# Two graph layers on one core: one fixed order of search matmuls in every attention step, and four smaller moves

## The chip, the core and the metric

The kernel runs on one core of a Trainium2 chip. The core has a matrix engine (TensorE, PE in the profile; its weight loads are listed as PEld), three engines that read and write on-chip memory (VectorE = DVE, ScalarE = ACT, GpSimd = POOL) and a queue (SyncE = SP) that issues all transfers of this kernel. Matrix products land in PSUM, which has eight banks of 512 fp32 columns; everything else lies in SBUF. Each engine takes its instructions strictly in the order of its own list and meets the others through semaphores.

The metric is the device time of one execution in microseconds (us). The kernel before was timed three times: 15735.61 us in the median (15734.61 to 15738.93).

## The reference

The inputs are `x` (3327 nodes x 128), a 0/1 matrix `adj` (3327 x 3327) and weights. There are two residual layers, each followed by a layer norm over the 128 features.

```python
# layer 0
cos = beta * (x @ x.T) / (|x| |x|^T + 1e-7)
x = layernorm(x + softmax(cos + (1 - adj) * -1e9) @ x)
# layer 1: n = 3327, d = 128 heads, h = 8 features per head
q, k, v = [(x @ W.T).reshape(d, n, h) for W in (Wq, Wk, Wv)]
a = softmax(einsum('dnh,dmh->dnm', q, k) * d**-0.5 + adj + adj)
x = layernorm(x + einsum('dnm,dmh->dnh', a, v).reshape(n, h*d) @ Wo.T)
```

Layer 1 dominates: 128 heads, each with a 3327 x 3327 score matrix that is built from only eight features.

## The kernel before

**Tiling.** Nodes are padded to 3328 = 26 tiles of 128 (`T` = 26). Query nodes are taken in nine blocks of three tiles (`QB` = 384 columns; the ninth has two tiles, 256 columns). A *unit* is one block times four heads; there are 9 x 32 = 288 units. A *step* is one unit times one tile of 128 key nodes, so a unit has 26 steps and the kernel has 7,488, of which 6,656 are full (384 columns). Each head's q and k carry 32 rows (eight features split into high and low parts and doubled), so the four heads of a unit lie in the four 32-row groups of PE, and products of different heads can run in PE at the same time. Those of one head share a row group and follow each other.

**Stages.** Layer 0 takes the first 718 us or so. It also turns each tile of `adj` and stores the turned tile to DRAM as `aT_s` (line 215, `adj_chunk`); the tile in SBUF has one buffer. Then a preparation stage (`prepare`, lines 794 to 823, 16 calls: eight groups of heads, k and q) loads 1.66 MB of q or k (`nat`, line 796), reorders it on POOL (798), transposes it on PE, splits it and writes it back (818). The attention loop (lines 872 to 943) runs from about 988 us to 15615 us, and a final stage multiplies with Wo, adds the residual and norms (lines 949 to 983).

**One step of the loop.** PE runs, in this order: the shift products of two heads (`shifts`, L690) into the two-bank tile `e_b`; a search; the score products of those heads (`scores`, L696); the shift products of the other two heads into two single-bank tiles `e_a`; another search; their scores; eight products that add 2 x adj to `e_a` (`add_adj`, L677); eight products that weigh the values of the step two earlier into `acc` (`weigh`, L707). ACT takes the exponential of `e_b` (L893) and of both `e_a` (L923). For the heads of `e_b`, adj is not added before the exponential: POOL multiplies by exp(2 adj) afterwards (L894).

**The searches.** Softmax needs each query row's maximum before its unit begins. So beside the steps of the running units PE forms the scores of the *next two* units only to find their maxima: per step a *pair* (two heads, 512 keys each, into the two-bank tile `m2`, L598, reduced by one DVE instruction, L613) and a *single* (one head, into `m1`, L634). `m2` and `m1` have one buffer each, so the next pair waits for the pair's reduction, and the next single for the single's. `max_steps` (568) writes the list of 52 pairs and singles for two units; 52 steps make a *round*. The list runs 33 steps ahead (`AHEAD` = 7): step s works on search place k = (s + 33) mod 52. Pairs take heads (0, 1) at places 0 to 12, (2, 3) at 13 to 38, (0, 1) at 39 to 51. Line 882 calls a place *early* when its pair has heads (0, 1). An early place runs the pair in the first slot (before the scores of `e_b`) and the single in the second; the others run the single first and the pair second. `e_b` always has heads (2, 3) and `e_a` (0, 1). Two pairs, at places 12 and 26, are made of four products of 256 keys for both units of the round (branch from line 618).

**Around the loop.** When a unit's 26 steps have been weighed, `take` copies `acc` (L718). At step 20 of the next unit (line 916) `values_turn` turns it on PE (L725) and `finish` (735) copies it out on ACT (L737), takes a reciprocal on DVE (L741), scales on POOL (L742) and stores to `o_s`. At place 26 or 51 (line 928) `shift_parts` reduces the maxima on DVE (L648) and splits them on POOL; three small turns (L663) at steps 22 to 24 bring them to PE's shape. A unit's k and q are loaded (`load_unit`, 517) two units ahead. For each new block, 26 turned adj tiles are loaded (`load_adj_tile`, 505) and exponentiated on ACT (L514).

**Who sets the order.** In layer 0 and layer 1 the lists of PE, ACT, DVE and POOL stand as written (`manual_schedule`). The SP list, and all lists in the final stage, are ordered by a scheduler.

**The final stage.** Per tile: load 128 rows of `o_s` and the residual, eight transposes, two copies (DVE and ACT), eight products, one DVE add into `hid` (978). After the 26 tiles `layernorm` (129) runs over all of them; the scheduler has put the statistics into the tile loop, the square root and 26 scalings (L141) behind it, and the whole output is then written.

## Time and profile before

| | us |
|---|---|
| median of three timed runs | 15735.61 |
| profiled execution, its own time | 15731.62 |
| its span on the core | 15729.8 |
| attention loop, first to last exponential L893 | 988.4 to 15613.0 |
| preparation stage | about 718 to 988 |
| final stage | about 15615 to 15729.8 |
| mean full step | 2.005 |
| mean step of the ninth block | 1.538 |

How to read it: the span is counted from the first instruction that the profile shows. A line such as "4143.72 0.50 PE L598 MATMUL m<-kx,qx ... x1" of the timeline is start, duration, engine, source line, operation, output and inputs, and how many equal instructions are merged; square brackets give idle time before it and what ended that. Matmuls are pipelined, so their shown durations overlap. Step times are differences between successive starts of the exponential L893, of which each step has one. "L141" is line 141 of the kernel.

### The profile page before, as it was taken

To read this page: it belongs to the slowest core of one execution; us is meant where nothing else is said; L and a number is where in the kernel's file an instruction comes from. 1 tells how busy PE (TensorE), PEld (TensorE's weight loads), DVE (VectorE), ACT (ScalarE), POOL (GpSimd) and SP (SyncE) were. 2 spreads that over 40 slices of the span, in tenths; PEclk is the share of its full clock that TensorE was granted. 3 is DMA by queue.
4 is the path that set the end of the run, shared out by engine and by line. 5 is a ranking of instruction groups with operands and counts; after the bars stand their busy time and mean duration, and the time that the engine had idled before them with its cause. 6 is when DMAs were issued, how large, how long until landed. Compare 5 with 4: busy or idle time off the path is not lost.

```text
span 15729.8 us, 508048 instructions
## 1 busy us (share of the span) xinstructions
PE 15442.3 (98%) x217532; PEld 6909.7 (44%) x217532; DVE 13882.2 (88%) x16261; ACT 12687.4 (81%) x24930; POOL 13894.1 (88%) x9571
## 2 busy tenths in 40 slices
PE   8879999999999999999999999999999999999999
PEld 6644444444444444444444444444444444444555
DVE  7679999999999999999999999999999999998775
ACT  7658888888888888888888888888888888888776
POOL 0059999999999999999999999999999999999886
PEclk9989999999999999999999999999999999999999
DMA  4451111111111111111111111111111111111112
GB/s 169 180 201 49 45 49 52 49 46 49 52 50 49 47 50 52 49 45 49 52 49 46 49 53 48 50 45 56 45 49 45 49 52 49 46 49 60 61 56 74
DMA packets 600521, 951.50 MB, mean 60 GB/s; under 512 B 283090, under 2 KB 515408, under 8 KB 557808
## 3 DMA queue, kind: packets, MB, share of 16 engines
q1 hardware_dynamic: 598256, 918.99, 18.0%
q8 instruction: 1703, 27.90, 0.7%
q14 instruction: 562, 4.60, 0.1%
HBM read 784.19 MB, written 134.61 MB: 58 GB/s over the span
## 4 chain that ended last, share of the span: by engine, by line
PE 91%; DVE 2%; ACT 1%; issue 0%; POOL 0%; DMA 0%; SPq 0%; ACTq 0%; DVEq 0%; POOLq 0%
PE acc L707 29%; PE ea L677 20%; PE m L598 15%; PE eb L690 12%; PE ea L690 9%; PE ea L696 2%; PE eb L696 2%; PE ea L663 1%; DVE mx L613 1%; PE ea L725 1%; DVE mx L634 1%; ACT pa L923 0%; PE pp L977 0%; POOL pb L894 0%; ACT pb L893 0%
## 5 line engine op out<-in xcount | busy, mean ns | idle before, releaser
L894 POOL TENSOR_TENSOR pb<-pb,eT 128x768 f32<-128x768 f32 (+1 forms) x7488 | 13206.6, 1781 | 752.7 <-ACT pb L893 557.7
L613 DVE TENSOR_REDUCE mx<-m 128x2 f32<-128x1024 f32 x6784 | 8271.6, 1219 | 506.9 <-PE eb L696 283.1
L893 ACT ACTIVATE pb<-eb 128x768 f32<-128x768 f32 (+1 forms) x7488 | 5895.6, 787 | 2509.9 <-PE eb L696 1716.6
L598 PE MATMUL m<-kx,qx 32*128 32x512 f32 (+1 forms) x23296 | 6774.5, 471 | 85.9 <-DVE mx L613 78.2
L923 ACT ACTIVATE pa<-ea 128x384 f32<-128x384 f32 (+1 forms) x14976 | 6339.0, 478 | 56.5 <-PE ea L677 43.5
L707 PE MATMUL acc<-pb,vt 128*9 128x384 f32 (+1 forms) x29952 | 5904.2, 474 | 0.1
L707 PE MATMUL acc<-pa,vt 128*9 128x384 f32 (+1 forms) x29952 | 5903.3, 474 | 0.0
L634 DVE TENSOR_REDUCE mx<-m 128x1 f32<-128x512 f32 x6400 | 4377.6, 684 | 682.2 <-PE m L598 316.3
L690 PEld LDWEIGHTS <-one 3*128 3x128 bf16 x29952 | 1508.1, 91 | 5553.9 <-issue 4650.8
L677 PE MATMUL ea<-aT,two 128*32 128x384 bf16 (+1 forms) x59904 | 3716.2, 325 | 0.0
L696 PE MATMUL eb<-qx,kx 32*128 32x384 f32 (+1 forms) x14976 | 3444.5, 452 | 0.0
L696 PE MATMUL ea<-qx,kx 32*128 32x384 f32 (+1 forms) x14976 | 3439.1, 437 | 0.0
L690 PE MATMUL ea<-cx,one 3*128 3x384 bf16 (+1 forms) x14976 | 3293.0, 322 | 2.3
L598 PEld LDWEIGHTS m<-kx,qx 32*128 32x128 f32 x23296 | 2813.9, 182 | 443.7 <-DVE mx L613 123.0
L690 PE MATMUL eb<-cx,one 3*128 3x384 bf16 (+1 forms) x14976 | 2462.7, 326 | 1.3 <-ACT pb L893 0.6
L707 PEld LDWEIGHTS acc<-pa,vt 128*9 128x9 f32 x29952 | 1416.7, 91 | 781.5 <-issue 0.3
L677 PEld LDWEIGHTS <-two 128*32 128x32 bf16 x59904 | 947.0, 95 | 1415.6 <-issue 1273.6
L696 PEld LDWEIGHTS eb<-qx,kx 32*128 32x128 f32 x14976 | 1461.7, 189 | 0.0
L696 PEld LDWEIGHTS ea<-qx,kx 32*128 32x128 f32 x14976 | 1433.1, 182 | 8.0 <-issue 3.0
L707 PEld LDWEIGHTS acc<-pb,vt 128*9 128x9 f32 x29952 | 1418.8, 91 | 0.6 <-POOL pb L894 0.6
L638 DVE TENSOR_REDUCE mx<-m 128x2 f32<-128x512 f32 x1088 | 747.9, 687 | 96.3 <-PE eb L696 38.2
L116 POOL MEMSET raw<- 128x1 f32 x26 | 2.4, 98 | 559.0 <-DVE mn L260 478.2
(126 smaller groups left out, 5253.8 us busy)
## 6 DMA issues: line engine op xcount, KB each, us to landing
kx<-kp_s SPq DMA_DIRECT2D x576, 832.0 KB
vn<-v_s SPq DMA_DIRECT2D x288, 416.0 KB
qx<-qp_s SPq DMA_DIRECT2D x1024, 48.0 KB
raw<-in_adj_dram SPq DMA_DIRECT2D x25, 1663.5 KB
aT_s<-aT SPq DMA_DIRECT2D x26, 832.0 KB
aT<-aT_s SPq DMA_DIRECT2D x208, 96.0 KB
q_s<-row SPq DMA_DIRECT2D x26, 512.0 KB
k_s<-row SPq DMA_DIRECT2D x26, 512.0 KB
```

The costliest lines, as they stand in the source:

```text
L598: nc.tensor.matmul(dst, u.qx[rows(a), q * P : (q + 1) * P], u.kx[rows(a), k0:k1], start=True, stop=True,)
L613: nc.vector.tensor_reduce(u.mx[:, h, qs[0], c], m, axis=AX.X, op=ALU.max)
L634: nc.vector.tensor_reduce(u.mx[:, a, qs[0], c : c + 1], m, axis=AX.X, op=ALU.max)
L638: nc.vector.tensor_reduce(u.mx[:, a, qs[0] : qs[1] + 1, c], m.rearrange("p (q k) -> p q k", q=2), axis=AX.X, op=ALU.max,)
L663: nc.tensor.matmul(dst[r], parts[u.i % 2][:, q, h], unit, start=start, stop=True, tile_position=(0, 32 * h), skip_group_check=True,)
L677: nc.tensor.matmul(e[r, : u.nq], two[:, r], aT[:, j, : u.nq], start=False, stop=True, tile_position=(0, 32 * c), skip_group_check=True,)
L690: nc.tensor.matmul(e[:, : u.nq], one[r], u.cx[r, : u.nq], start=True, stop=False, skip_group_check=True)
L696: nc.tensor.matmul(e[:, : u.nq], u.kx[rows(a), j * P : (j + 1) * P], u.qx[rows(a), : u.nq], start=False, stop=stop, skip_group_check=True,)
L707: nc.tensor.matmul(acc[32 * h : 32 * h + H + 1, : u.nq], u.vt[:, h, j], pts[h // 2][:, h % 2, : u.nq], start=(j == 0), stop=(j == T - 1), ...
L893: nc.scalar.activation(pt_b[:, :, : u.nq], e_b[:, :, : u.nq], AF.Exp)
L894: nc.gpsimd.tensor_tensor(pt_b[:, :, : u.nq], pt_b[:, :, : u.nq], eT[:, j, : u.nq].unsqueeze(1).to_broadcast([P, 2, u.nq]), ALU.mult,)
L923: nc.scalar.activation(pt_a[:, h, : u.nq], e[:, : u.nq], AF.Exp)
```

## The change

The search list, the slots, and four separate moves:

1. **Search order.** In all full units the pair always stands in the first slot and the single in the second. The heads of the step follow: `e_a` takes the pair's heads and `e_b` the other two, so places 13 to 38 now have heads (2, 3) in `e_a` and (0, 1) in `e_b`. `weigh` picks each head's weights from a dictionary. One single moves in the list, so that no single shares a head with its place's pair (two places did before: 12 and 38). The ninth block keeps single first and the old roles.
2. **Values.** `values_turn` moves from step 20 to step 8; `finish` is split: the copy (`leave`) stays at step 8, the reciprocal, scaling and store come at step 9.
3. **Turned adj.** `aT_s` is laid out by block, so a tile's load reads 768 consecutive bytes per partition in place of three pieces of 256, and the store in layer 0 writes 3,328 pieces of 256 bytes in place of 128 of 6,656.
4. **Preparation.** The loads of q and k are written two calls ahead; adj tile loads of the first block come seven at a time between calls instead of 26 at once. In the SP list, what changes is that 22 adj loads no longer stand before the third load of `nat`, and that the store of a unit's output stands before the wait for the next `vn` load rather than after it.
5. **Last norm.** The layer norm of the final stage runs tile by tile inside the loop; the first 20 tiles of the output are written when they are done, the last six at the end. In the lists, each tile's square root stands on ACT behind its copy; reciprocal and scaling stand on DVE behind the next tile's copy.

```diff
-    aT_s = dram.tile([T, P, T, P], BF16, name="aT_s")
+    aT_s = dram.tile([NB, P, T, QT * P], BF16, name="aT_s")
...
     def layernorm(dst: bass.AP, src: bass.AP):
-        stats = small.tile([P, T, nc.vector.BN_STATS_DIM], F32, name="ln_stats", bufs=1)
...
+        stats = small.tile([P, nc.vector.BN_STATS_DIM], F32, name="ln_stats")
+        mv = small.tile([P, nc.vector.BN_AGGR_DIM], F32, name="ln_mv")
+        rstd = small.tile([P, 1], F32, name="ln_rstd")
+        nc.vector.bn_stats(stats, src)
+        nc.vector.bn_aggr(mv, stats)
+        nc.vector.tensor_scalar(rstd, mv[:, 1:2], EPS, None, op0=ALU.add)
         nc.scalar.activation(rstd, rstd, AF.Sqrt)
         nc.vector.reciprocal(rstd, rstd)
-        for t in range(T):
...
+        nc.vector.tensor_scalar(
+            dst, src, mv[:, 0:1], rstd, op0=ALU.subtract, op1=ALU.mult
+        )
...
-                nc.sync.dma_start(aT_s[t], u.aT)
+                q = t % QT
+                nc.sync.dma_start(aT_s[t // QT][:, :, q * P : (q + 1) * P], u.aT)
...
-            nc.sync.dma_start(
-                aT[:, j, :w].rearrange("p (q n) -> p q n", n=P),
-                aT_s[b * QT : b * QT + w // P, :, j].rearrange("q p n -> p q n"),
-            )
+            nc.sync.dma_start(aT[:, j, :w], aT_s[b][:, j, :w])
...
-            ones = one(u, hi, full[13:] + [left]) + one(u, lo, full[12:] + [left])
+            last = one(w, hi, full[12:] + [left])
+            ones = one(u, hi, full[13:] + [left]) + last[:1] + one(u, lo, full[12:] + [left])
...
-            ones += one(w, lo, full[13:] + [left])
             pairs += [(w, lo, *k) for k in full[:13]]
-            ones += one(w, hi, full[12:] + [left])
+            ones += one(w, lo, full[13:] + [left]) + last[1:]
...
+        def search(step):
+            if step is not None:
+                (max_pair if len(step[1]) == 2 else max_single)(*step)
...
-                    pts[h // 2][:, h % 2, : u.nq],
+                    pts[h][:, : u.nq],
...
-        def finish(u, src):
-            of = sm.tile([P, QT, 4, H + 1], F32, name="of")
-            nc.scalar.copy(of[:, : u.nt].rearrange("p q h r -> p (q h r)"), src[:, : 36 * u.nt])
-            by = of.rearrange("p q h r -> p h q r")[:, :, : u.nt]
+        def leave(u, src):
+            u.of = sm.tile([P, QT, 4, H + 1], F32, name="of")
+            nc.scalar.copy(u.of[:, : u.nt].rearrange("p q h r -> p (q h r)"), src[:, : 36 * u.nt])
+
+        def finish(u):
+            by = u.of.rearrange("p q h r -> p h q r")[:, :, : u.nt]
...
+                works = [(g, *w) for g in range(NG) for w in ((k_s, kp_s), (q_s, qp_s))]
...
+                def load_heads(i):
+                    if i < len(works):
+                        nat = work.tile([P, HG, T * H], F32, name="nat")
+                        nc.sync.dma_start(nat, heads(works[i][1])[works[i][0]])
+                        nats.append(nat)
...
+                    load_heads(i + 2)
...
-                    early = pair is not None and pair[1] == (0, 1)
+
+                    full = pair is not None and width(units[pair[0]][0]) == QB
+                    first = pair if full else single
+                    late = single if full else pair
+                    hs_a = pair[1] if full else (0, 1)
+                    hs_b = tuple(h for h in range(4) if h not in hs_a)
...
-                    shifts(u, b01, (2, 3))
-                    if early:
-                        max_pair(*pair)
-                    elif single is not None:
-                        max_single(*single)
-                    scores(u, j, b01, (2, 3), True)
+                    shifts(u, b01, hs_b)
+                    search(first)
+                    scores(u, j, b01, hs_b, True)
...
-                    shifts(u, e_a, (0, 1))
-                    if early:
-                        max_single(*single)
-                    elif pair is not None:
-                        max_pair(*pair)
-                    scores(u, j, e_a, (0, 1), False)
+                    shifts(u, e_a, hs_a)
+                    search(late)
+                    scores(u, j, e_a, hs_a, False)
...
-                    if j == T - 6 and done is not None:
+                    if j == 8 and done is not None:
                         values_turn(done, free, False)
-                        copies.append(lambda: finish(done, free))
+                        copies.append(lambda: leave(done, free))
+                    if j == 9 and done is not None:
+                        copies.append(lambda: finish(done))
...
-                    todo.append((u, j, (pt_a, pt_b)))
+                    pts = {}
+                    for x in range(2):
+                        pts[hs_a[x]], pts[hs_b[x]] = pt_a[:, x], pt_b[:, x]
+                    todo.append((u, j, pts))
...
-            nc.vector.tensor_add(hid[:, t, :], pp, x1)
-        res = big.tile([P, T, D], F32, name="res")
-        layernorm(res, hid)
-        rf = res.rearrange("p t d -> p (t d)")
+            hid = work.tile([P, D], F32, name="hid1")
+            nc.vector.tensor_add(hid, pp, x1)
+            layernorm(res[:, t, :], hid)
+            if t == HALF - 1:
+                nc.sync.dma_start(node_blocks(out, slice(0, P), HALF * D), rf[:, : HALF * D])
         for part, width in node_parts():
-            nc.sync.dma_start(node_blocks(out, part, width), rf[part, :width])
+            dst = node_blocks(out, part, width)
+            nc.sync.dma_start(dst[:, HALF * D :], rf[part, HALF * D : width])
```

## The prediction

> **What bounds the kernel now.** I read the page first: engine shares, then the chain.
>
> ```profile
> PE 15442.3 (98%) x217532; PEld 6909.7 (44%) x217532; DVE 13882.2 (88%) x16261; ACT 12687.4 (81%) x24930; POOL 13894.1 (88%) x9571
> PE acc L707 29%; PE ea L677 20%; PE m L598 15%; PE eb L690 12%; PE ea L690 9%; PE ea L696 2%; PE eb L696 2%; PE ea L663 1%; DVE mx L613 1%; PE ea L725 1%; DVE mx L634 1%; ACT pa L923 0%; PE pp L977 0%; POOL pb L894 0%; ACT pb L893 0%
> ```
>
> PE looks busy nearly all the time and holds the chain. But products of different heads overlap, and quick and slow steps look equally full, so the share doesn't say how fast a step could be. The groups show who works beside PE on the searches:
>
> ```profile
> L613 DVE TENSOR_REDUCE mx<-m 128x2 f32<-128x1024 f32 x6784 | 8271.6, 1219 | 506.9 <-PE eb L696 283.1
> L634 DVE TENSOR_REDUCE mx<-m 128x1 f32<-128x512 f32 x6400 | 4377.6, 684 | 682.2 <-PE m L598 316.3
> ```
>
> A full step costs DVE 1219 + 684 = 1903 ns, close to the mean step of 2.005 us. So I went to the timeline, at places 46 and 47 of a round, where the pair stands first already:
>
> ```profile
> 4143.18 0.50 PE L598 MATMUL m<-kx,qx 32*128 32x512 f32 x2
> 4143.72 0.50 PE L598 MATMUL m<-kx,qx 32*128 32x512 f32 x1
> 4143.73 1.23 DVE L613 TENSOR_REDUCE mx<-m 128x2 f32<-128x1024 f32 x1
> 4144.87 0.68 DVE L634 TENSOR_REDUCE mx<-m 128x1 f32<-128x512 f32 x1
> 4145.24 0.50 PE L598 MATMUL m<-kx,qx 32*128 32x512 f32 x2
> 4145.60 0.49 PE L598 MATMUL m<-kx,qx 32*128 32x512 f32 x1
> 4145.78 1.23 DVE L613 TENSOR_REDUCE mx<-m 128x2 f32<-128x1024 f32 x1 [0.23 <-PE eb L696]
> ```
>
> See a loop over two steps. A single can't start before the previous single is reduced: 4143.72 follows the end of a reduction at 4143.66. From that single PE needs 1.52 us to the next pair (4145.24), the pair reaches DVE 0.54 later (4145.78), DVE takes 1.14 to the single's reduction and 0.68 for it, 0.06 later a single may start: 1.52 + 0.54 + 1.14 + 0.68 + 0.06 = 3.94 us for two steps, 1.97 each. Slow and quick steps alternate (2.05 and 1.88 here).
>
> Next, all starts of L893, averaged by place over the eight full blocks; a round of 52 sums to 104.28 us:
>
> | places | order | mean interval |
> |---|---|---|
> | 40 to 51 | pair first | 1.971 |
> | 7 to 10 | pair first | 1.970 |
> | 14 to 25 | single first | 1.970 |
> | 33 to 36 | single first | 1.970 |
> | 11, 12, 13 | change of order | 2.068, 2.378, 1.873: 0.41 above 3 x 1.970 |
> | 37, 38, 39 | change back | 2.160, 2.288, 1.865: 0.40 above |
> | 0 to 6 | values, shift turns | 0.59 above 7 x 1.970 |
> | 26 to 32 | the same | 0.42 above |
>
> Both orders have one rhythm, and 1.81 us of a round lie at changes of order and at unit ends. The change back, in the timeline:
>
> ```profile
> 4128.23 1.22 DVE L613 TENSOR_REDUCE mx<-m 128x2 f32<-128x1024 f32 x1
> 4129.01 0.33 PE L690 MATMUL eb<-cx,one 3*128 3x384 bf16 x2
> 4129.50 0.50 PE L598 MATMUL m<-kx,qx 32*128 32x512 f32 x2 [0.15 <-DVE mx L613]
> 4130.04 1.23 DVE L613 TENSOR_REDUCE mx<-m 128x2 f32<-128x1024 f32 x1 [0.60 <-PE m L598]
> ```
>
> Two pairs follow each other. The second needs `m2`, which DVE frees only at 4129.45; PE stands, with the scores of `e_b` queued behind the pair, and DVE then idles 0.60 us.
>
> **Part 1, the order: -90 us.** With the pair always first, no two pairs or two singles meet, so 0.81 us a round lose their cause, and the two shared-head places go with them. What stays: the pair of four products of 256 keys at place 12, first as before, and its twin at place 26, now first too. At place 12 the scores behind it start 0.19 us after the pair and not 0.03 to 0.04 (4075.12 against 4074.93), so up to about 0.1 us stays at each. I take 0.70 us x 128 rounds = 90 us. Ends: 0.81 x 128 = 104 if the wide pairs hide in slow steps; 51 (one change's worth) if half returns where the roles swap. The rhythm I leave at 1.97: same instructions, and the loop above names no head.
>
> **Part 2, values: -15 us.** `values_turn` holds PE for 0.22 us (L725 at 3063.09, `add_adj` at 3063.31). The reciprocal blocks DVE:
>
> ```profile
> L741 DVE RECIPROCAL rec<-of x288: 203/228/232, 1083.8 to 15616.8; 128x12 f32<-128x12 f32 x128, 128x8 f32<-128x8 f32 x16
>   ACT of L737: 127.8, 196
> ```
>
> DVE waits 0.65 us each in 196 of 288 cases, with the next reductions queued behind. One step later the copy is done, so the wait goes; 0.22 on PE and 0.23 on DVE stay. Places 0 to 2 and 26 to 28 now exceed the rhythm by 0.39 and 0.19, mean 0.29 a unit. After: as little as 0.05 (PE's 0.22 less the 0.17 by which the single waits in a slow step), at most 0.45 (both in the loop). I take 0.23, 0.06 less: 256 x 0.06 = 15 us; ends -61 and +41. The shift turns (three of 0.07) and `shift_parts` (0.24 on DVE) don't move. POOL's scaling, 0.36, goes from step 20 to step 9, away from the 1.2 us of `values` at step 14; where POOL lags most (1.35 us), `weigh` still comes some two steps later, so POOL hides either way. The store joins SP before its wait for `vn`; nobody reads it before the final stage.
>
> **Part 3, adj layout: nothing in the loops, counted in part 4.** A store in layer 0 now has 3,328 pieces of 256 bytes. Pieces of that size take 18 ns each in the adj loads, those of 6,656 bytes 255: 3328 x 18 / 16 = 3.7 us on 16 engines against 128 x 255 / 16 = 2.0. Its cover: the tile is stored at 150.0 and next written at 166.9. Without cover, 26 x 1.7 = 44 us; I keep 0 to +5. The loads in the loop lie five steps ahead of their use.
>
> The Trainium skill ("DMA: Bandwidth & Descriptors", Specifications) says that below 512 bytes a transfer engine does read-modify-write; the rule speaks against this store. Taken as a doubling of the piece, an estimate from that page, a store would take 7.5 us, still inside the 17 us of cover: the same sum. The trace has only reads at 256 bytes; its stores of 96-byte pieces took 12 ns.
>
> **Part 4, preparation: -4 us.** The windows:
>
> ```profile
> 720.00:800.00 80.00, 21.28 (x98) 18.53 (x98) 15.55 (x29) 12.83 (x23) 11.82 (x4) 0.56 1.00 328
> 960.00:990.00 30.00, 17.45 (x99) 13.32 (x100) 19.36 (x32) 9.81 (x18) 5.91 (x6) 0.61 0.88 312
> ```
>
> The last two columns are DMA share and GB/s. Though POOL waits 41 us for the third `nat`, the transfer engines are full: loading earlier moves bytes, it doesn't remove any. What shrinks is the adj load: 26 x (384 x 18 - 128 x 36) / 16 = 3.7 us (36 ns for 768 bytes is an estimate between rows of 27 ns for 512 and 39 for 832). Ends: -10 if the idle DMA time at the end goes too (12% of the last 30 us, 3% of the 80 before: 6 us), +10 if a late load costs half of the 20 us for which POOL waited for one at 805.
>
> **Part 5, last norm: -10 us.**
>
> ```profile
> 15714.92 6.75 DVE L141 TENSOR_SCALAR res<-hid,ln_mv,ln_rstd 128x128 f32<-128x128 f32 x26
> 15721.45 1.12 SPq L983 DMA_DIRECT2D out_dram<-res  x3
> ```
>
> 25 of 26 scalings leave the end: 25 x 0.26 = 6.5 us. The write of 1.66 MB lay from 15722.2 to 15728.5; six tiles' share is 0.39 MB, so I take 2.5 us for 6.3: 3.8 less. Per tile DVE gains 0.18 + 0.2 + 0.26 us and a wait for ACT's square root of about 0.3, all in the 2.06 us for which it idles before each add; ACT has 2.77. If not covered, 26 x 0.9 = 23 us more. SP's early write, 1.3 MB, stands ahead of loads that are two tiles (6.7 us) early. Ends: -11 to -6.
>
> **Sum.** -90 - 15 + 0 - 4 - 10 = -119 us on a span of 15729.8, so 15611. The profiled execution's own time is 1.8 above its span, and the median 4.0 above that execution: 15735.6 - 119 = 15616.6.
>
> **Rivals.**
>
> *The cost comes back.* Where roles swap, or where the values now fall, the rhythm slips as much as at the old changes. For: a loop that spans two steps passes a delay on. Against: `shift_parts` puts 0.24 us more on DVE at places 26 and 51, and the intervals 51 and 0 together take 3.942 us, no more than two steps of 1.97. Then only parts 4 and 5 stay: 15735.6 - 14 = 15722, no measurable change.
>
> *Larger gain.* The unit ends fall into slow steps, where the single has 0.17 us to spare, and changes cost nothing: 104 + 61 + 10 + 11 = 186, so 15550. For: DVE no longer stands behind the copy. Against: in places 0 to 2, with the pair first, the event costs 0.39, the dearer of the two.
>
> *Slower: the swapped roles.* `e_b` with heads (0, 1) behind a pair of (2, 3) has never run. If those steps all took the slow pace (2.07 against 1.97), 26 x 128 x 0.10 = 333 us would be lost against 119 won: 15950. It decides from 119 / 3328 = 0.036 us a step. For: nothing shown; only that half of all full steps are of an unseen kind. Against: single-first steps with other row groups together keep the same 1.970.
>
> **How the numbers follow.** Forecast 0.65, larger gain 0.14, cost comes back 0.13, slower 0.08. About 0.2% (31 us) can be told from no change: below 15704 is faster. So faster 0.79, same 0.13, slower 0.08. The forecast's own bounds: low -104 - 61 - 10 - 11 = -186; high -51 + 41 + 5 + 10 - 6 = -1, improbable together. The range 15540 to 15715 holds the forecast nearly whole and the larger gain, and leaves out the slower case and most of the third.
>
> **What would show it.** Right: a round of about 103.4 us, no interval over 2.2 at places 12 and 38, all places' rhythm 1.97; waits of L741 for L737 near nothing; the last write of 0.4 MB and some 4 us from the last PE work to its issue gone by half or more; preparation within 10 us of 270. Wrong: intervals above 1.99 at places 14 to 25 or 40 to 51 (swapped or unswapped rhythm changed), a rise at steps 8 and 9 above 0.45, or a rhythm below 1.95, which would mean that the loop of 3.94 us isn't what binds.

## The result, and the profile after

Over four runs each the median went from 15735.11 us (15732.48 to 15738.93) to 15624.67 us (15621.11 to 15632.83): ratio 0.9931, 95% interval 0.9919 to 0.9943. The forecast was 15616.6, 8 us too low, with a range of 15540 to 15715. The profiled execution took 15621.11 us with a span of 15619.3, at a granted clock of 0.992 as before.

The kernel after has new line numbers: the pair's search is L605, the single's L626, both products L590, shifts L686, scores L692, `add_adj` L673, `weigh` L703, `values_turn` L721, the copy in `leave` L733, the reciprocal L739. The page's engine shares and its chain of work that ended last:

```profile
PE 15363.4 (98%) x217532; PEld 6915.8 (44%) x217532; DVE 13899.2 (89%) x16311; ACT 12602.2 (81%) x24955; POOL 13880.8 (89%) x9571
PE 93%; DVE 0%; ACT 0%; issue 0%; DMA 0%; SPq 0%; POOL 0%; POOLq 0%; ACTq 0%; DVEq 0%
PE acc L703 30%; PE ea L673 21%; PE m L590 16%; PE eb L686 12%; PE ea L686 10%; PE ea L692 2%; PE ea L659 1%; PE ea L721 1%; PE eb L692 1%; PE pp L994 0%; ACT pa L934 0%; DVE oT L147 0%; ACT pb L905 0%; DMA qp_s<-low 0%; PE tp L157 0%
```

The shares hardly differ from before. What differs is the chain: the searches on DVE had 1% each of it before, now they stand in no row of it. The groups of the two searches (the last columns are busy us, mean ns, and the idle time just before them with its main releaser):

```profile
L605 DVE TENSOR_REDUCE mx<-m 128x2 f32<-128x1024 f32 x6784 | 8312.3, 1225 | 968.3 <-PE eb L692 571.4
L626 DVE TENSOR_REDUCE mx<-m 128x1 f32<-128x512 f32 x6400 | 4360.4, 681 | 258.5 <-PE m L590 238.7
```

Instructions and durations are the same (1219 and 684 ns before). DVE's idle time moved from the single's search (682.2 to 258.5 us) to the pair's (506.9 to 968.3). Their sum even rose by 38 us in a run that is 110 us shorter: idle time of an engine doesn't say what a run could save.

The timeline at places 38 and 39 of a round, where the order used to change back, shows the cause gone:

```profile
4106.21 1.23 DVE L605 TENSOR_REDUCE mx<-m 128x2 f32<-128x1024 f32 x1
4107.35 0.68 DVE L630 TENSOR_REDUCE mx<-m 128x2 f32<-128x512 f32 x1
4107.63 0.34 PE L686 MATMUL eb<-cx,one 3*128 3x384 bf16 x2
4107.64 0.50 PE L590 MATMUL m<-kx,qx 32*128 32x512 f32 x2
4107.97 0.35 PE L686 MATMUL ea<-cx,one 3*128 3x384 bf16 x2
4108.09 0.50 PE L590 MATMUL m<-kx,qx 32*128 32x512 f32 x1
4108.18 1.23 DVE L605 TENSOR_REDUCE mx<-m 128x2 f32<-128x1024 f32 x1
4108.28 0.81 ACT L905 ACTIVATE pb<-eb 128x768 f32<-128x768 f32 x1 [0.40 <-PE m L590]
4108.51 0.51 PE L673 MATMUL ea<-aT,two 128*32 128x384 bf16 x8
4108.85 0.49 PE L703 MATMUL acc<-pb,vt 128*9 128x384 f32 x2
4109.32 0.68 DVE L626 TENSOR_REDUCE mx<-m 128x1 f32<-128x512 f32 x1
4109.60 0.34 PE L686 MATMUL eb<-cx,one 3*128 3x384 bf16 x2
```

Pair, single (here one of twice 256 keys), pair, single: before its next pair DVE stands for 0.15 us, where it stood for 0.60 us between two pairs. The loop of the prediction can be read off again: the single at 4108.09 follows the end of the reduction at 4108.03, the next pair starts 1.51 us later (4109.60, with the shifts of `e_b`), and a pair reaches DVE 0.54 us after its start (4107.64 to 4108.18). One step of PE is also seen here: 0.34 for the pair, 0.12 of waiting for `m1`, 0.42 for the single with its scores, 0.34 for `add_adj`, 0.75 for `weigh`: 1.97.

Starts of the exponential of `e_b` averaged by place over the eight full blocks, as in the prediction (excess over 1.970 us a step):

| | before | after |
|---|---|---|
| round of 52 steps | 104.28 | 103.45 |
| rhythm, places 18 to 25, single first before, swapped roles after | 1.970 | 1.969 |
| rhythm, places 43 to 50 | 1.970 | 1.970 |
| places 0 to 6 and 26 to 32 (unit ends) | 0.59, 0.42 | 0.23, 0.28 |
| places 11 to 13 and 37 to 39 (changes of order) | 0.41, 0.40 | 0.07, -0.01 |
| places 14 to 16 and 40 to 42 (after: step 8) | 0.07, 0.10 | 0.19, 0.19 |
| first to last exponential of `e_b` | 14624.5 | 14523.2 |
| last exponential to the end | 116.9 | 105.3 |
| start to the first exponential | 988.4 | 990.9 |

So -101.3 us in the loop, -11.6 behind it, +2.4 ahead of it. The reciprocal's waits, from the trace's answer on that line:

```profile
L739 DVE RECIPROCAL rec<-of x288: 194/219/221, 1065.0 to 15517.9; 128x12 f32<-128x12 f32 x128, 128x8 f32<-128x8 f32 x16
  ACT of L733: 50.6, 2
```

196 waits of 127.8 us in total became 2, both at the last two units of the loop (23.8 us at 15490.8 and 26.8 at 15517.9). Before, too, had three long ones there, 50.7 us together. So 77 us of DVE's waits are gone, 193 of 0.40 us on average; the prediction's 0.65 us each spread the three long ones over all 196. The experiments show what that was worth.

The last tiles, from the timeline:

```profile
15612.63 3.69 SPq L1002 DMA_DIRECT2D out_dram<-res  x3
15613.65 0.29 DVE L996 TENSOR_TENSOR hid<-pp,x1r 128x128 f32<-128x128 f32 x1 [1.05 <-PE pp L994]
15615.15 0.35 DVE L139 TENSOR_SCALAR res<-hid,ln_mv,ln_rstd 128x128 f32<-128x128 f32 x1
```

From the last add to the last scaling's end there are 1.85 us; one scaling in place of 26 stands at the end. DVE still waits 1.05 us before each add, 2.06 before: the norm of a tile took about a microsecond of that gap and the tiles' period stayed 3.355 us.

### The profile page after: what moved, and what is told of

The parts are those of the page before. It is cut to its first block, busy times and chain, and to the rows that moved or that the text cites. A ratio compares the mean times of both kernels' runs of the same rounds, so it can differ in the third digit from the quotient of the medians.

```text
span 15619.3 us, 508226 instructions
## 1 busy us (share of the span) xinstructions
PE 15363.4 (98%) x217532; PEld 6915.8 (44%) x217532; DVE 13899.2 (89%) x16311; ACT 12602.2 (81%) x24955; POOL 13880.8 (89%) x9571
## 4 chain that ended last, share of the span: by engine, by line
PE 93%; DVE 0%; ACT 0%; issue 0%; DMA 0%; SPq 0%; POOL 0%; POOLq 0%; ACTq 0%; DVEq 0%
PE acc L703 30%; PE ea L673 21%; PE m L590 16%; PE eb L686 12%; PE ea L686 10%; PE ea L692 2%; PE ea L659 1%; PE ea L721 1%; PE eb L692 1%; PE pp L994 0%; ACT pa L934 0%; DVE oT L147 0%; ACT pb L905 0%; DMA qp_s<-low 0%; PE tp L157 0%
## 5 line engine op out<-in xcount | busy, mean ns | idle before, releaser
L605 DVE TENSOR_REDUCE mx<-m 128x2 f32<-128x1024 f32 x6784 | 8312.3, 1225 | 968.3 <-PE eb L692 571.4
L590 PE MATMUL m<-kx,qx 32*128 32x512 f32 (+1 forms) x23296 | 6873.9, 472 | 81.2 <-DVE mx L605 72.2
L703 PE MATMUL acc<-pb,vt 128*9 128x384 f32 (+1 forms) x29952 | 5901.9, 474 | 0.1
L703 PE MATMUL acc<-pa,vt 128*9 128x384 f32 (+1 forms) x29952 | 5901.8, 474 | 0.0
L626 DVE TENSOR_REDUCE mx<-m 128x1 f32<-128x512 f32 x6400 | 4360.4, 681 | 258.5 <-PE m L590 238.7
L686 PEld LDWEIGHTS <-one 3*128 3x128 bf16 x29952 | 1469.0, 91 | 5630.9 <-issue 4654.9
L673 PE MATMUL ea<-aT,two 128*32 128x384 bf16 (+1 forms) x59904 | 3715.0, 325 | 0.0
L692 PE MATMUL eb<-qx,kx 32*128 32x384 f32 (+1 forms) x14976 | 3422.2, 453 | 0.0
L692 PE MATMUL ea<-qx,kx 32*128 32x384 f32 (+1 forms) x14976 | 3326.5, 434 | 0.0
L590 PEld LDWEIGHTS m<-kx,qx 32*128 32x128 f32 x23296 | 2825.5, 182 | 320.9 <-DVE mx L605 84.4
L686 PE MATMUL ea<-cx,one 3*128 3x384 bf16 (+1 forms) x14976 | 2745.2, 324 | 1.0
L686 PE MATMUL eb<-cx,one 3*128 3x384 bf16 (+1 forms) x14976 | 2464.5, 326 | 1.4 <-ACT pb L905 0.6
L703 PEld LDWEIGHTS acc<-pa,vt 128*9 128x9 f32 x29952 | 1411.9, 91 | 398.9
L703 PEld LDWEIGHTS acc<-pb,vt 128*9 128x9 f32 x29952 | 1411.7, 91 | 386.8 <-issue 0.7
L673 PEld LDWEIGHTS <-two 128*32 128x32 bf16 x59904 | 945.2, 94 | 1364.4 <-issue 1170.2
L692 PEld LDWEIGHTS eb<-qx,kx 32*128 32x128 f32 x14976 | 1432.6, 188 | 0.0
L692 PEld LDWEIGHTS ea<-qx,kx 32*128 32x128 f32 x14976 | 1395.8, 182 | 7.4 <-issue 4.2
```

The costliest lines, as they stand in the source:

```text
L590: nc.tensor.matmul(dst, u.qx[rows(a), q * P : (q + 1) * P], u.kx[rows(a), k0:k1], start=True, stop=True,)
L605: nc.vector.tensor_reduce(u.mx[:, h, qs[0], c], m, axis=AX.X, op=ALU.max)
L626: nc.vector.tensor_reduce(u.mx[:, a, qs[0], c : c + 1], m, axis=AX.X, op=ALU.max)
L673: nc.tensor.matmul(e[r, : u.nq], two[:, r], aT[:, j, : u.nq], start=False, stop=True, tile_position=(0, 32 * c), skip_group_check=True,)
L686: nc.tensor.matmul(e[:, : u.nq], one[r], u.cx[r, : u.nq], start=True, stop=False, skip_group_check=True)
L692: nc.tensor.matmul(e[:, : u.nq], u.kx[rows(a), j * P : (j + 1) * P], u.qx[rows(a), : u.nq], start=False, stop=stop, skip_group_check=True,)
```

## The experiments: each part alone

Times below are medians; where a kernel ran once, its profile is what it was run for. "Round", "rhythm" and "excess" are those of the table above.

**order_only: part 1 alone, on the kernel before.** Its core:

```diff
-                    early = pair is not None and pair[1] == (0, 1)
+                    full = pair is not None and width(units[pair[0]][0]) == QB
+                    first = pair if full else single
+                    late = single if full else pair
+                    hs_a = pair[1] if full else (0, 1)
+                    hs_b = tuple(h for h in range(4) if h not in hs_a)
...
-                    shifts(u, b01, (2, 3))
+                    shifts(u, b01, hs_b)
...
-                    shifts(u, e_a, (0, 1))
+                    shifts(u, e_a, hs_a)
```

> The kernel before with part 1 alone (pair first everywhere, roles follow, no shared heads); values stay at step 20, norm, layout and preparation as before. Theory (the gain sits where the order changed): the excess of 0.81 us at places 11 to 13 and 37 to 39 falls to about 0.07, the rest of the round stays within 0.1, so about 0.75 x 128 = 96 us less than before, ratio 0.994. Rival (the gain needs the values moved as well, since the loop spans two steps and only shifts the excess to places 0 to 2 and 26 to 28): less than 40 us, with the excess at places 0 to 6 and 26 to 32 above 1.2 us a round.

Measured: 15619.6 us (15611.34 to 15630.7, four runs) against 15731.37 for before, ratio 0.9929 (0.9914 to 0.9944). The round is 103.44 us, the loop 14517.6: 106.9 us less than before. Places 11 to 13 keep 0.06, places 37 to 39 nothing. This one part makes the whole gain of the loop; the round of the full change (103.45) is no shorter.

**values_only: part 2 alone.**

```diff
-                    if j == T - 6 and done is not None:
+                    if j == 8 and done is not None:
                         values_turn(done, free, False)
-                        copies.append(lambda: finish(done, free))
+                        copies.append(lambda: leave(done, free))
+                    if j == 9 and done is not None:
+                        copies.append(lambda: finish(done))
```

> The kernel before with part 2 alone (values turned at step 8, copied out there, the reciprocal one step later). Theory (only DVE's wait behind the copy goes; 0.22 us on PE and 0.23 on DVE stay): 5 to 25 us less than before, waits of the reciprocal for the copy near nothing. Rival (the values are most of the gain, because DVE stood 128 us in that wait): 60 us or more less.

Measured: 15720.96 us (15715.89 to 15726.14, ten runs), ratio 0.9993 (0.9983 to 1.0002): the interval includes no change. No reciprocal waits for the copy in the loop any more; the round goes from 104.28 to 104.20. Places 0 to 6 and 26 to 32 fall to 0.24 and 0.28, but places 14 to 16 and 40 to 42 rise from 0.07 and 0.10 to 0.20 each. The round lost 0.08 us and the unit ends 0.49: most of the cost moved with the work.

**norm_only: part 5 alone.**

```diff
-            nc.vector.tensor_add(hid[:, t, :], pp, x1)
-        res = big.tile([P, T, D], F32, name="res")
-        layernorm(res, hid)
+            nc.vector.tensor_add(hid, pp, x1)
+            layernorm(res[:, t, :], hid)
+            if t == HALF - 1:
+                nc.sync.dma_start(node_blocks(out, slice(0, P), HALF * D), rf[:, : HALF * D])
```

> The kernel before with part 5 alone (norm by tiles, output written in two goes). Theory: 10 to 12 us less, all of it after the last exponential; the final stage about 105 us against 116.8. Rival (the root and reciprocal in the tile loop hold the next tile): tile period above 3.36 us and a gain under 5 us.

Measured: 15725.39 us (15716.37 to 15733.14, ten runs), ratio 0.9998 (0.9988 to 1.0007). The interval can't tell it from nothing; the profile can, since this part has a stage of its own: from the last exponential to the end 106.1 us against 116.9 in before, 116.1 in order_only and 116.4 in values_only. All kernels with this part lie at 104.9 to 106.1.

**prep_layout: parts 3 and 4 alone.**

```diff
-                nc.sync.dma_start(aT_s[t], u.aT)
+                q = t % QT
+                nc.sync.dma_start(aT_s[t // QT][:, :, q * P : (q + 1) * P], u.aT)
...
+                    load_heads(i + 2)
```

> The kernel before with parts 3 and 4 (adj by block, loads two ahead, adj loads spread). Theory (the transfer engines are full in this stage, so order can't help, and spread small loads delay the heads' loads a little): the first exponential 0 to 4 us later than before's 988.4, layer 0 unchanged within 2 us, total within 5 us of before. Rival (the loss of 2.4 us in the changed kernel came from profile to profile scatter, and the layout saves its 3.7 us): first exponential 2 to 6 us earlier.

Measured: 15728.51 us (15724.42 to 15735.27, ten runs), ratio 1.0 (0.999 to 1.0009). The first exponential starts at 986.0. That start scatters: with the old preparation it lies at 988.4, 995.2, 989.8 and 996.3 (before and the three kernels above), with the new one between 986.0 and 997.3 in ten profiles. Counted from layer 0's last store of `v_s`, the stage takes 269.7 to 271.3 us with the old preparation (278.6 in norm_only) and 267.9 to 273.9 with the new. So the 2.4 us by which this run starts earlier lie in the rival's band, but well inside the scatter: no gain can be read. The windows of after, columns as in the prediction, show the same:

```profile
720.00:800.00 80.00, 28.64 (x114) 19.56 (x115) 18.43 (x33) 15.74 (x29) 14.78 (x5) 0.54 1.03 350
960.00:990.00 30.00, 16.93 (x90) 12.61 (x90) 20.67 (x35) 7.99 (x15) 5.24 (x5) 0.67 0.82 292
```

The early window moves more (350 GB/s, 328 before) and the late one less (292, 312 before): bytes moved forward, while the last 30 us got no shorter.

## The experiments: what the order and the values are worth

**roles_fixed: the heads of `e_a` and `e_b` stay as they were.** Only the constant order remains of part 1.

```diff
-                    hs_a = pair[1] if full else (0, 1)
+                    hs_a = (0, 1)
```

> The changed kernel with the pair first everywhere but the old roles: heads (2, 3) always in the first half, so at places 13 to 38 the pair's heads are those of the scores behind it. Theory (products of one row group follow each other, so the roles are what makes the fixed order affordable): in the first half scores wait for the whole pair, 0.43 us; in the second the single shares a head with the scores behind it; a step at places 13 to 38 takes 2.15 to 2.3 us, 26 x 128 x 0.2 to 0.3 = 650 to 1000 us more in all. Rival (PE has slack behind the two-step loop and the fixed order alone is enough): those places stay within 0.03 of 1.97.

Measured: 16102.12 us (one run; before 15734.52), so +368 against before and some 480 against after (loop 15001.8 against 14523.2). Places 18 to 25 and 33 to 36 go at 2.11 a step, slow 2.24 and quick 1.98 in turn; the rhythm at places 43 to 50 stays at 1.969. The timeline of a quick step (place 21) and the start of the slow one behind it:

```profile
4077.26 0.34 PE L686 MATMUL eb<-cx,one 3*128 3x384 bf16 x2
4077.30 0.53 PE L590 MATMUL m<-kx,qx 32*128 32x512 f32 x2
4077.55 0.49 PE L590 MATMUL m<-kx,qx 32*128 32x512 f32 x1
4077.66 0.34 PE L692 MATMUL eb<-qx,kx 32*128 32x384 f32 x2
4077.87 1.23 DVE L605 TENSOR_REDUCE mx<-m 128x2 f32<-128x1024 f32 x1 [0.41 <-PE ea L686]
4077.89 0.33 PE L692 MATMUL ea<-qx,kx 32*128 32x384 f32 x1
4078.10 0.81 ACT L905 ACTIVATE pb<-eb 128x768 f32<-128x768 f32 x1 [0.60 <-PE m L590]
4078.81 0.87 ACT L934 ACTIVATE pa<-ea 128x384 f32<-128x384 f32 x2
4079.73 0.32 PE L686 MATMUL ea<-cx,one 3*128 3x384 bf16 x1
4080.38 0.51 PE L673 MATMUL ea<-aT,two 128*32 128x384 bf16 x8
```

The pair of heads (2, 3) and the scores of `e_b` for the same two heads use the same two groups of 32 rows. They no longer overlap: the scores start 0.36 us behind the pair (4077.66 against 4077.30), in after 0.03 (4107.67 against 4107.64), and the exponential starts 0.84 us after the shifts of `e_b` (4078.10 against 4077.26), in after 0.65 (4108.28 against 4107.63). A second place is shared too: the single has the head of one of the scores behind it, and these start 0.34 us after it (4077.89 against 4077.55). From there PE needs 0.65 us from the second shift of `e_a` to `add_adj` (4079.73 to 4080.38), where after's single needs 0.42.

Both delays lie in a loop over two steps that the prediction didn't have, between PE and ACT: 0.84 from the shifts of `e_b` to their exponential, 0.71 to the exponentials of `e_a`, 0.87 for these, 0.05 to the second shift into the tile that they free, 0.65 to `add_adj`, 1.09 to the next shifts of `e_b` (as in after, 0.34 + 0.75). That is 4.21 us, or 2.11 a step, the rhythm measured. In the steps at places 18 to 25 that second shift follows the exponential by 0.051 to 0.052 us in the middle 80% of them. So the roles are no decoration of the constant order, they are what makes it possible; how the cost divides between the pair's shared heads and the single's, this run doesn't show. My size was too large: the round grew by 3.74 us, 0.14 for each of the 26 steps.

**old_list: the list of singles as before,** in which a single meets its own pair's head at two places of a round.

```diff
-            last = one(w, hi, full[12:] + [left])
-            ones = one(u, hi, full[13:] + [left]) + last[:1] + one(u, lo, full[12:] + [left])
+            ones = one(u, hi, full[13:] + [left]) + one(u, lo, full[12:] + [left])
...
+            ones += one(w, lo, full[13:] + [left])
...
-            ones += one(w, lo, full[13:] + [left]) + last[1:]
+            ones += one(w, hi, full[12:] + [left])
```

> The changed kernel with the search list of before, so at places 12 and 38 the single shares a head with its pair and with the scores behind it; order and roles as changed. Theory (one shared head puts the single's 0.43 us in front of its head's scores): 0.1 to 0.35 us more at places 11 to 13 and 37 to 39 each, 0.2 to 0.7 us a round, 25 to 90 us. Rival (a slow step hides it): within 0.05 a round.

Measured: 15618.45 us (one run; after 15617.74 on the same chip), round 103.44 against 103.42. Place 38 rises to 2.15 and places 39 and 40 are 1.87 and 2.07, where after_again has 1.99, 1.95 and 1.99; half of the delay of 0.17 us stays. At place 12 the same delay is given back by place 15, and places 26 to 32 come out 0.10 lower (0.18 against 0.28), so that the round is the same. The list of singles is worth nothing that a round shows by itself; all of part 1 is the order with its roles.

**no_values: everything but part 2**, beside a second measurement of the changed kernel, **after_again**, on the same chip.

```diff
-                    if j == 8 and done is not None:
+                    if j == T - 6 and done is not None:
                         values_turn(done, free, False)
-                        copies.append(lambda: leave(done, free))
-                    if j == 9 and done is not None:
-                        copies.append(lambda: finish(done))
+                        copies.append(lambda: finish(done, free))
```

> Parts 1, 3, 4 and 5 without part 2 (values at step 20, not split). Theory (part 2 gives nothing once the order is fixed, and costs 3 us in the ninth block): 0 to 8 us less than the whole change, round 103.4 to 103.5, ninth block 1.537 to 1.538 a step. Rival (part 2 is worth the 15 us that it was put at): 10 us or more over the whole change.

> The changed kernel itself, beside no_values on the same chip. All theories: 105 to 120 us less than before, round 103.4 to 103.5, ninth block 1.541 to 1.542 a step.

Measured: 15619.8 us without part 2 (15612.17 to 15622.98, five runs; ratio 0.9928, 0.9914 to 0.9941), 15617.74 with it (15617.1 to 15620.32, five runs; ratio 0.9927, 0.9915 to 0.994). Rounds 103.41 and 103.42, loops 14516.8 and 14517.9. On top of the order, part 2 is worth nothing that can be measured. Yet its waits are there; DVE's waits in the loop (us in total, times, longest), no_values:

```profile
DVE rec L737 <- ACT of L733: 73.8, 173, 1.4
DVE rec L737 <- POOL parts L654: 20.7, 110, 0.3
```

94.5 us of waiting on the engine that the loop runs through, and next to no time in them, as the next run shows.

**values_20: the work stays at step 20, only the reciprocal comes a step later.**

```diff
-                    if j == 8 and done is not None:
+                    if j == T - 6 and done is not None:
...
-                    if j == 9 and done is not None:
+                    if j == T - 5 and done is not None:
```

> The changed kernel with the values turned at step 20 again, but still split (copy at 20, reciprocal at 21). It separates the place from the split. Theory (DVE's wait behind the copy cost nothing on the path once the order is fixed; the 0.22 us on PE is what counts, wherever it stands): the round is within 0.08 us of 103.44, the value that both the order alone and the whole change gave, with no wait of the reciprocal for the copy. Rival (the wait was worth 0.06 a unit, and step 8 is a worse place that eats it): the round falls to 103.3 or less.

Measured: 15611.69 us (one run; after_again 15617.1 to 15620.32), round 103.38, no wait of the reciprocal in the loop. This parts the wait from the place. Excess by places:

| kernel | wait for the copy | 0 to 2 | 26 to 28 | 14 to 16 | 40 to 42 |
|---|---|---|---|---|---|
| order_only | yes | 0.33 | 0.19 | -0.06 | 0.01 |
| values_20 | no | 0.33 | 0.18 | -0.07 | 0.02 |
| after | no | -0.03 | 0.15 | 0.19 | 0.19 |

With the wait or without it, step 20 costs the same. The round is 0.03 us under that of no_values and 0.06 under that of order_only, 4 to 8 us in all; the changed kernel's own two profiles differ by 0.03. Moving to step 8 takes 0.36 and 0.04 off the unit ends, 0.20 a unit, and puts on 0.25 and 0.18, 0.21 a unit. That is the 0.22 us for which `values_turn` holds PE, seen at step 8 in the timeline of after:

```profile
4060.42 0.44 PE L692 MATMUL ea<-qx,kx 32*128 32x384 f32 x2
4060.85 0.40 PE L721 MATMUL ea<-nine,ot 128*32 128x36 f32 x24
4061.06 0.51 PE L673 MATMUL ea<-aT,two 128*32 128x384 bf16 x8
4061.61 0.68 DVE L626 TENSOR_REDUCE mx<-m 128x1 f32<-128x512 f32 x1
4062.15 0.34 PE L686 MATMUL eb<-cx,one 3*128 3x384 bf16 x2
4062.69 1.23 DVE L605 TENSOR_REDUCE mx<-m 128x2 f32<-128x1024 f32 x1 [0.41 <-PE eb L692]
...
4064.43 0.22 DVE L739 RECIPROCAL rec<-of 128x12 f32<-128x12 f32 x1
```

`add_adj` starts 0.22 us late, so does everything of PE behind it, and DVE waits 0.41 us for the next pair. The reciprocal at 4064.43 follows a reduction without a gap, and the intervals there (places 16 and 17) are 1.95 and 1.98: DVE's 0.22 us costs nothing. Values_20 is the lowest single time of all, but 5 to 9 us under five runs of after is within what one run scatters; no version here beats the changed kernel by a difference that I can measure.

## The experiments: is it the loop that binds?

**single_half: the single's search looks at 256 of its 512 keys,** the products stay.

```diff
-                nc.vector.tensor_reduce(u.mx[:, a, qs[0], c : c + 1], m, axis=AX.X, op=ALU.max)
+                nc.vector.tensor_reduce(u.mx[:, a, qs[0], c : c + 1], m[:, :256], axis=AX.X, op=ALU.max)
```

> The changed kernel, with the single's reduction on DVE reading 256 of its 512 keys, so half of those keys are left out of the maximum and DVE takes about 0.4 us for it, not 0.68. No other instruction changes. Theory (the loop of 3.94 us over two steps sets the rhythm): the loop falls to 3.66, under what PE needs by itself, so the rhythm falls to the quick step's 1.88 or to POOL's pace of about 1.90; the round falls by 3 to 5 us, 350 to 600 us in all. Rival (PE's own work sets 1.97 on average, quick and slow steps being a matter of packing): the rhythm stays within 0.02 of 1.970.

Measured: 15279.08 us (one run; before 15734.52). The rhythm is 1.900 us (1.88 and 1.92 in turn), the round 100.74. The group and one round of all engines (PE, PEld, DVE, ACT, POOL busy us, granted clock, DMA share, GB/s):

```profile
L626 DVE TENSOR_REDUCE mx<-m 128x1 f32<-128x256 f32 x6400 | 2661.4, 416 | 400.9 <-PE m L590 374.0
```

```profile
4000.00:4100.74 100.74, 100.74 (x1500) 41.98 (x1488) 83.86 (x109) 84.83 (x168) 98.77 (x67) 1.00 0.15 49
```

The single's reduction is 0.265 us shorter, and 0.07 us a step came of it. So the reduction is in what binds: PE, 98% busy on the page in both kernels, was done 345 us earlier than in after without one matmul less. But if the loop of 3.94 us alone bound, 0.265 off it would give 1.84 a step; something else stops at 1.90. POOL is busy for 98.77 of these 100.74 us (99.25 of a round of 103.45 in after), so it lies close. But the timeline has a loop of just this length without it, the one between PE and ACT that roles_fixed stretched:

```profile
4097.32 0.34 PE L686 MATMUL eb<-cx,one 3*128 3x384 bf16 x2
4097.96 0.81 ACT L905 ACTIVATE pb<-eb 128x768 f32<-128x768 f32 x1 [0.33 <-PE eb L692]
4098.67 0.87 ACT L934 ACTIVATE pa<-ea 128x384 f32<-128x384 f32 x2
4099.59 0.50 PE L590 MATMUL m<-kx,qx 32*128 32x512 f32 x1
4100.02 0.51 PE L673 MATMUL ea<-aT,two 128*32 128x384 bf16 x8
4101.11 0.34 PE L686 MATMUL eb<-cx,one 3*128 3x384 bf16 x2
```

0.64 to the exponential of `e_b`, 0.71 to those of `e_a`, 0.87 for them, 0.05 to the second shift of `e_a` with the single right behind it (4099.59), 0.43 to `add_adj`, 1.09 to the shifts of `e_b`: 3.79 us for two steps, 1.90 each. At places 43 to 50 (middle 80% of the steps) that shift follows the exponential by 0.050 to 0.052 us here, by 0.053 to 0.108 in after; the single follows the reduction that frees `m1` by 0.055 us in after (10th percentile and median alike), by 0.175 to 0.177 here. So in after the loop through DVE is the one that is always tight; here it has slack, and the loop through ACT is tight. No run changed the second loop alone.

**weigh_mid: `weigh` of two steps ago is emitted between the scores of `e_b` and `e_a`,** not at the end of the step, and **weigh_mid_lag3: the same, a step later.** The aim was to shorten the 1.52 us that PE needs from a single to the next pair.

```diff
+                    if s >= LAG:
+                        weigh_old()
                     e_a = new_a()
...
-                if s >= LAG:
-                    w = todo.pop(0)
-                    weigh(*w)
...
-        AHEAD, LAG = 7, 2
+        AHEAD, LAG = 7, 3      # weigh_mid_lag3 only
```

> The changed kernel with the eight products that weigh the values moved from the end of a step to its middle, between the first half's scores and the second half's shifts; the same instructions, still two steps behind. Theory (two-step loop): from the single to the next pair PE then needs 0.64 us less, the loop falls from 3.94 to 3.30 us and stops binding. PE packs a little worse (two halves of 0.48 us for one stretch of 0.91), so PE needs about 1.92 a step, DVE 1.89, POOL about 1.90: rhythm 1.90 to 1.95, 130 to 450 us less. Rival (PE's own work sets the rhythm): the worse packing costs 0.05 a step, 2.02, some 300 us more.

> The same as weigh_mid, but weighing three steps behind, not two. In weigh_mid the values' weights from POOL have about 1.1 us to spare, and POOL lags up to 1.4 us after the unit ends and after the values are copied. Theory: where weigh_mid shows excess at places 0 to 3, 21 to 24, 27 to 30 and 47 to 50, this one shows up to 0.3 us less at each, 10 to 100 us in all; the rhythm is the same. Rival (POOL's lag is never met by PE): both within 10 us.

Measured: 16767.08 us (16753.31 to 16790.27, four runs), ratio 1.0658 (1.0642 to 1.0674), and 16776.95 (16766.8 to 16785.27, four runs), ratio 1.0665 (1.0647 to 1.0682). The rhythm is 2.085 in both, so a later `weigh` doesn't help and the rhythm isn't set by data that come late. Against 130 to 450 us less in the forecast, weigh_mid took 1033 more than before; I had expected nothing as large. The timeline of a steady step of weigh_mid (the shifts of `e_b` stand just ahead of the pair, those of `e_a` ahead of the single):

```profile
5002.21 0.33 PE L686 MATMUL eb<-cx,one 3*128 3x384 bf16 x2
5002.65 0.50 PE L703 MATMUL acc<-pb,vt 128*9 128x384 f32 x2
5003.41 0.34 PE L686 MATMUL ea<-cx,one 3*128 3x384 bf16 x2
5003.85 0.51 PE L673 MATMUL ea<-aT,two 128*32 128x384 bf16 x8
5004.29 0.34 PE L686 MATMUL eb<-cx,one 3*128 3x384 bf16 x2
```

From the single to the next pair PE now takes 0.88 us (5003.41 to 5004.29) and not 1.52, as was meant. But it goes from block to block in 0.44 + 0.76 + 0.44 + 0.44 = 2.08 us with no wait in it, and so has become the bound itself. In after the first block takes 0.34 into the next shifts, here 0.44 into `weigh`; `add_adj` takes 0.34 into `weigh` there, here 0.44 into the shifts. `weigh` and `add_adj` use the array at its full height, shifts, searches and scores in groups of 32 rows. I read this as a price of about 0.1 us for each passage between the two kinds, of which the new order has four in a step in place of two; two blocks agree on it, but no run has the passages alone. The Trainium skill ("TensorEngine Tiling (Array Packing)", Key Properties) says that a change of the tiling mode drains TensorE. The two 0.10 us fit that; the drain itself isn't seen in the trace.

The waits of PE show the rest, for `acc` and for POOL's product (us in total, times, longest):

```profile
PE acc L703 <- ACT ot L714: 125.3, 154, 1.1
PE acc L703 <- POOL pb L914: 94.3, 106, 0.9
```

These waits lie at a few steps of each unit (in weigh_mid_lag3 that for POOL's product is no smaller, 106.0 us): the round is 7.64 us above after's, 52 x 0.115 = 6.0 of it rhythm.

## Why the prediction was right, and where it wasn't

- *The bound: a loop over two steps, not PE's share.* Held where it was used. The rhythm stayed at 1.97 in all of order_only, values_20, old_list and after, whichever heads are in front, and single_half moved it by a change on DVE alone. It was incomplete: the loop is closely followed by a second one through ACT at 1.90, which the prediction doesn't have.
- *Part 1, -90 us.* The mechanism holds: intervals of 2.378 and 2.288 at places 12 and 38 became 1.88 and 1.98, and order_only alone gave -106.9. The size was off by 17: I left 0.1 us at each of the two pairs of four products, and took 0.70 a round. Places 11 to 13 keep 0.07 and those at 37 to 39 nothing; the round lost 0.84. My end of 104 was the better value: "if the wide pairs hide in slow steps".
- *Part 2, -15 us.* This is the step that failed. I charged 0.29 us a unit to PE's 0.22 and the wait of the reciprocal together, and let the wait's share go. The wait, 0.40 us on average in the loop and not the 0.65 that I read, costs nothing that can be measured where it was (values_20 against order_only: the same 0.33 and 0.19, 0.18); PE's 0.22 costs 0.20 to 0.21 in either place. Left were 0 us on top of the order. Values_only's 0.08 a round (some 10 us, in an interval that includes no change) is what it may give with the old order, and it doesn't add. That the sum came out so near is thus partly two errors that cancel: 17 us too few in part 1, 15 too many here.
- *Part 3, 0.* Held. Layer 0 stored its last `v_s` at 717.9 us, before at 718.7.
- *Part 4, -4 us.* Not to be told from the start's own scatter of 10 us; nothing speaks for it. "Loading earlier moves bytes" held, the shorter adj load didn't show.
- *Part 5, -10 us.* Held: -11.6, and -10.8 in norm_only. That the norm of a tile fits into the 2.06 us before each add was right: 1.05 are left.
- *The rival that the cost comes back* fell: the swapped roles run at 1.969, and values moved at no loss. *The larger gain* fell with the unit ends: what stands there is PE's work. *Slower by swapped roles* fell, but it looked at the right place: roles_fixed shows that row groups shared between the searches and the scores behind them cost 0.14 us a step, and the swap is what keeps them apart.
- *The signs.* The round came to 103.45 (about 103.4 foretold), the step 8 to 9 rise to 0.18 to 0.25 (below 0.45), layer 0's last store to the first exponential to 273.0 (270). Place 15 at 2.24 lies above the 1.99 that was to speak against the swapped roles; it is the values' step, since order_only, with the same roles, has 2.03 there and 1.91 ahead of it. The sign was badly set in any case: single places alternate, and before itself has 2.07 and 1.87 in turn at places 40 to 50.
- *Sum.* Order -107, values 0, preparation 0, norm -11: -118, against -119 predicted and -110.5 in the profiled span, -113.6 in that of after_again. The difference lies within the start's scatter and the last block, whose step took 1.5416 against 1.5379 us (832 steps, 3 us). That rise is there in after, after_again and old_list, less in no_values (1.5404), where I had expected none; norm_only, whose loop is that of before, has 1.5399, so a part of it at least is not from the loop's order. Its cause stays open.

## What to carry to other kernels

Where two engines pass two single buffers to and fro, write the loop down with its times and look for the places where its order breaks: one constant order was worth all that the loop gained, and it needed the partners in a step to be chosen so that they never share rows of the array. A wait that the profile lists, even 90 us of it on an engine in the loop, proves nothing until removing only that wait shortens a round. Here 0.22 us of work on PE cost 0.20 to 0.21 in either place where it was put. When a loop is loosened, look for the next one before you size the gain: here it lay 0.07 us a step below. Before you reorder matmuls to shorten a path, count how often the order changes between full-height and row-grouped products.

## What I had not expected of the hardware

- A block of row-grouped products took 0.44 us ahead of full-height ones and 0.34 ahead of others of its kind, and a block of full-height ones likewise: about 0.1 us a passage by my reading. An order with two more of them in a step ran 6.6% longer than before.
- Stores in pieces of 256 bytes took 20 ns a piece in layer 0 (mean of the transfer records), reads of that size 18. The doubling that the prediction worked out from the Trainium skill's rule for pieces under 512 bytes ("DMA: Bandwidth & Descriptors", Specifications) doesn't show here.
- A second limit lies close under the first: with a reduction 0.265 us shorter a step fell only from 1.97 to 1.90 us, and not to the 1.84 of the loop. The second is again a loop over two steps, through ACT and the two tiles of `e_a`, 3.79 us long.
